# Turning the adjacency by DMA from a bf16 scratch in DRAM, and centring the layer norm on VectorE, in a four-layer graph-attention kernel

## Chip, cores and metric

The kernel runs on one core of a Trainium2 chip. The metric is the device time of one execution in microseconds (us); lower is better. The engines are named as the profile names them: PE is TensorE (PEld its weight loads), DVE is VectorE, ACT is ScalarE, POOL is GpSimd, SP is SyncE, which here only issues DMAs.

## What is computed

There are 16 graphs of 1024 nodes with 256 features, and an adjacency of 1024 x 1024 int32 for each. Four layers follow one another; each takes the layer norm of the nodes, cuts it off at 0, attends over the neighbours and adds the result to the nodes. Cut to what matters:

```python
for layer in range(4):
    h = maximum((x - mean(x)) / sqrt(var(x) + 1e-5), 0)      # per node
    Wh = h @ W                                               # 256 -> 256
    e = act(Wh @ a_src [:, None] + Wh @ a_dst [None, :])     # 1024 x 1024
    att = softmax(where(adj != 0, e, -inf))                  # layer 1: exp(-leaky), no softmax
    x = x + post(att @ Wh)                                   # layer 3: 4 heads of 64, own layer norm
```

The kernel needs the adjacency turned: its masks hold, for a block j of 128 neighbours on the partitions, all 1024 rows i along the free axis.

## The kernel before

A guard decides at the end, from a few statistics, whether a general path has to run; in this case it does not, and all time is in `short_path`.

A batch is one graph. Two Python generators, `stream(0)` and `stream(1)`, take the even and the odd batches; a small loop interleaves them by the virtual times that they yield, with the second one 120 units behind. So while one stream is in layer 3 the other is in layers 0 to 2. This gives the order in which the program is written. The framework's scheduler then places each engine's instructions: an engine may be given a later instruction early, where what it needs is ready in the scheduler's own model. Every engine then runs its own list strictly in order, and waits on semaphores.

What one batch does:

- `load(b)` (L95) brings the nodes `x_b` (one DMA on SP's queue, L98) and the mask. Each of 8 row blocks of the adjacency is fetched by a DMA on POOL's queue that also casts int32 to bf16 (L105), into one of 3 buffers `adj_i`, two ahead (`AHEAD`). ACT squares it with a sum (L116, tile `wide`; the sums serve the guard). PE turns its eight 128 x 128 blocks into one PSUM tile of the pool `misc` (L121), which has 3 buffers that the kernel shares with all other turns, and ACT copies that tile as uint8 into the mask (L122). The load of batch b + 2 is spread over layer 3 of batch b: one step after each of its 8 head halves (L421).
- `project(l, ...)` (L215), for pairs of 128-node tiles, 4 pairs in each layer: DVE takes mean and variance (L220, L221) and scales the variance (L211), POOL raises it to the power -1/2 (L212). ACT negates the mean (L224), then ACT computes relu(x - mean) for each tile (L228, tile `above`), PE turns it (L232), ACT copies it out of PSUM (L234, `hT`), PE multiplies with W (L238), and ACT and DVE evict it (L288 to L292, in layer 3 L308 to L316).
- `weigh` (L244): DVE makes the attention weights (L257), eight instructions of 128 x 512 for each half, each with the mask of one j. Three layers need 16 of them, layer 3, with its four heads, 64.
- `attend` (L320) multiplies weights and values on PE (L340) and ends in `finish`: ACT and DVE (L273 to L276), then POOL adds to `x_b` (L277). The next layer's `project` of a pair follows two tiles later, and its statistics (L220) wait for L277.
- Layer 3 (from L372): PE L416, ACT L420 copies the sums, PE turns them back (L425), and DVE and POOL do its layer norm (L381 to L396). Two stores of the result go out on SP's queue (L441).

The pieces that the change touches read:

```python
        def fetch(i: int):
            fetched[i] = adjs.tile([P, N], BF, name="adj_i")
            nc.gpsimd.dma_start(fetched[i], adj[b, ts(i, P), :])
```

```python
        minus_mean = small.tile([P, 2], F32, name="minus_mean")
        nc.scalar.mul(minus_mean, mv[:, :, 0], -1.0)
```

Of the kernel before, what the change touches and what calls it, by code (L numbers as in the profile page):

```python
# [31 lines left out]
F32 = mybir.dt.float32  # L32
BF = mybir.dt.bfloat16
# [3 lines left out]
AF = mybir.ActivationFunctionType  # L37
ALU = mybir.AluOpType
AX = mybir.AxisListType

P = 128
# [17 lines left out]
def short_path(ctx: ExitStack, tc: tile.TileContext, ins: dict, out: bass.AP, bad: bass.AP):  # L59

    nc = tc.nc
    x, adj = ins["x"], ins["adj"]
    B, N, D = x.shape
    H, T, E = ins["L3_a_src"].shape
    NI = N // P
# [5 lines left out]
    AHEAD = 2  # L71
    LAG = 120.0

    const = ctx.enter_context(tc.tile_pool(name="const", bufs=1))
    nodes = ctx.enter_context(tc.tile_pool(name="nodes", bufs=3))
    adjs = ctx.enter_context(tc.tile_pool(name="adjs", bufs=3))
    wide = ctx.enter_context(tc.tile_pool(name="wide", bufs=3))
    psum = ctx.enter_context(tc.tile_pool(name="psum", bufs=2, space=bass.MemoryType.PSUM))

    ident = const.tile([P, P], F32, name="ident")  # L80
    make_identity(nc, ident)
    ident_b = const.tile([P, P], BF, name="ident_b")
    nc.vector.tensor_copy(ident_b, ident)
    minus_half = const.tile([P, 1], F32, name="minus_half")
    nc.vector.memset(minus_half, -0.5)
    ones = const.tile([P, P], F32, name="ones")
# [2 lines left out]
    squares = const.tile([P, B, NI], F32, name="squares")  # L89
# [3 lines left out]
    xs, masks = {}, {}  # L93

    def load(b: int):  # L95

        xs[b] = nodes.tile([P, NI, D], F32, name="x_b")
        nc.sync.dma_start(xs[b], x[b].rearrange("(i p) f -> p i f", p=P))  # L98
        masks[b] = nodes.tile([P, NI, N], U8, name="mask")
        fetched = {}  # L100

        def fetch(i: int):

            fetched[i] = adjs.tile([P, N], BF, name="adj_i")
            nc.gpsimd.dma_start(fetched[i], adj[b, ts(i, P), :])  # L105

        for i in range(AHEAD):
            fetch(i)
        yield
        for i in range(NI):  # L110
            if i + AHEAD < NI:
                fetch(i + AHEAD)
            adj_i = fetched.pop(i)

            every = wide.tile([P, N], BF, name="wide")
            nc.scalar.activation(  # L116
                every, adj_i, AF.Square, bias=minus_half, accum_out=squares[:, b, i : i + 1]
            )
            turned = psum.tile([P, NI, P], BF, name="misc", bufs=3)
            for j in range(NI):  # L120
                nc.tensor.transpose(turned[:, j, :], adj_i[:, ts(j, P)], ident_b)  # L121
            nc.scalar.copy(masks[b][:, :, ts(i, P)], turned)  # L122
            yield


# [8 lines left out]
    bias = const.tile([P, D], F32, name="bias")  # L134
# [4 lines left out]
    for _ in load(0):  # L139
        pass  # L140
# [5 lines left out]
    with tc.tile_pool(name="prep", bufs=2) as prep:  # L146
# [30 lines left out]
        for l, form in enumerate(forms):  # L177
            n = EXT[l] // 3
# [25 lines left out]
    small = ctx.enter_context(tc.tile_pool(name="small", bufs=6))  # L204
# [4 lines left out]
    def inverse_root(var: bass.AP, n: int, eps: float, scale: float = 1.0) -> bass.AP:  # L209
        r = small.tile([P, n], F32, name=f"rstd{n}")  # L210
        nc.vector.tensor_scalar(r, var, scale, eps, op0=ALU.mult, op1=ALU.add)  # L211
        nc.gpsimd.tensor_tensor(r, r, minus_half.to_broadcast([P, n]), op=ALU.pow)  # L212
        return r

    def project(l: int, xb: bass.AP, pair: int, evict):  # L215

        mv = small.tile([P, 2, nc.vector.BN_AGGR_DIM], F32, name="mv")
        for n in range(2):
            stats = small.tile([P, nc.vector.BN_STATS_DIM], F32, name="stats")
            nc.vector.bn_stats(stats, xb[:, 2 * pair + n, :])  # L220
            nc.vector.bn_aggr(mv[:, n, :], stats)  # L221
        rstd = inverse_root(mv[:, :, 1], 2, LN_EPS)
        minus_mean = small.tile([P, 2], F32, name="minus_mean")
        nc.scalar.mul(minus_mean, mv[:, :, 0], -1.0)  # L224
        turned = psum.tile([P, NK, 2 * P], F32, name="misc", bufs=3)
        for n in range(2):
            above = work.tile([P, D], F32, name="above")
            nc.scalar.activation(  # L228
                above, xb[:, 2 * pair + n, :], AF.Relu, bias=minus_mean[:, n : n + 1]
            )  # L230
            for k in range(NK):
                nc.tensor.transpose(turned[:, k, ts(n, P)], above[:, ts(k, P)], ident)  # L232
        hT = wide.tile([P, NK, 2 * P], F32, name="hT")
        nc.scalar.copy(hT, turned)  # L234
        for n in range(2):
            projected = psum.tile([P, D + EXT[l]], F32, name="projected")
            for k in range(NK):
                nc.tensor.matmul(  # L238
                    projected, hT[:, k, ts(n, P)], W[l][:, k, :],
                    start=(k == 0), stop=(k == NK - 1),  # L240
                )
            evict(2 * pair + n, projected, rstd[:, n : n + 1])
# [36 lines left out]
    def batch(b: int):  # L279
        xb, mask = xs.pop(b), masks.pop(b)  # L280
        coming = load(b + 2) if b + 2 < B else iter(())

        def begin(l: int):
# [36 lines left out]
        def attend(l: int, V: bass.AP, finish, then: int):  # L320
# [12 lines left out]
            for i in range(NI):  # L333
                t = next(weighing[1], None)
                if t:
                    yield t
                acc = psum.tile([P, HALF], F32, name="acc", bufs=3)[:, : D + 1]
                w = halves[i // NG]
                for j in range(NI):
                    nc.tensor.matmul(  # L340
                        acc, w[:, j, ts(i % NG, P)], V[:, j, : D + 1],
                        start=(j == 0), stop=(j == NI - 1),
                    )
                finish(i, acc)
                yield 3.6
                if i % 2 == 0 and i > 0:
                    project(then, xb, i // 2 - 1, following[1])
                    yield 4.0
            project(then, xb, NI // 2 - 1, following[1])
            yield 4.0  # L350
            return following[0]
# [12 lines left out]
        for pair in range(NI // 2):  # L364
            project(0, xb, pair, evict)
            yield 4.0
# [81 lines left out]
    def stream(first: int):  # L448
        if first:
            for _ in load(first):  # L450
                yield 2.0
        for b in range(first, B, 2):
            yield from batch(b)
# [314 lines left out]
def tile_gat4(  # L768
# [27 lines left out]
    nc.vector.memset(ones, 1.0)  # L796
    n_bad = flags.tile([1, 1], I32, name="n_bad")
    short_path(tc, ins, out, bad)
    with tc.tile_pool(name="flag_psum", bufs=1, space=bass.MemoryType.PSUM) as psum:
        bads = psum.tile([1, 1], F32, name="bads")  # L800
# [39 lines left out]
```

## Time and profile before

| | |
|---|---|
| median of 3 runs | 3347.73 us (3344.62 to 3347.99) |
| the profiled execution | 3347.73 us, of which its span 3346.1 us |
| mean granted PE clock | 0.985 of full speed |
| PE, DVE, ACT, POOL busy | 3098.2, 2381.6, 1235.0, 1082.2 us |
| PE busy from 0 to 50 us | 22.6 us |
| PE busy from 3030 to the end, 316.1 us | 272.6 us |
| adjacency DMAs (L105) | 128 of 256 KB written; 3.8 us from issue to landing |
| PE turns of the adjacency (L121) | 1024, 88.0 us busy |
| ACT copies into the mask (L122) | 128, 1005 ns each |
| ACT negated mean (L224), centring (L228) | 256 of 202 ns, 512 of 502 ns |

The span is what the profile resolves; 1.6 us of the execution lie around it. Busy time counts an engine from the start of an instruction to its end, overlaps once. A wait is the idle time of an engine before an instruction, put down to what ended last. The chain of waits is followed back from the last instruction, at each step to what released it.

### The profile page before, as it was taken

To read this page: it belongs to the slowest core of one execution; us is meant where nothing else is said; L and a number is where in the kernel's file an instruction comes from. 1 tells how busy PE (TensorE), PEld (TensorE's weight loads), DVE (VectorE), ACT (ScalarE), POOL (GpSimd) and SP (SyncE) were. 2 spreads that over 40 slices of the span, in tenths; PEclk is the share of its full clock that TensorE was granted. 3 is DMA by queue.
4 is the path that set the end of the run, shared out by engine and by line. 5 is a ranking of instruction groups with operands and counts; after the bars stand their busy time and mean duration, and the time that the engine had idled before them with its cause. 6 is when DMAs were issued, how large, how long until landed. Compare 5 with 4: busy or idle time off the path is not lost.

```text
span 3346.1 us, 38658 instructions
## 1 busy us (share of the span) xinstructions
PE 3098.2 (93%) x13702; PEld 2124.8 (64%) x13702; DVE 2381.6 (71%) x5628; ACT 1235.0 (37%) x2849; POOL 1082.2 (32%) x1286
## 2 busy tenths in 40 slices
PE   6899998999989999899998999989999899998987
PEld 5765755667656675666756667566675666756662
DVE  4567686777767777677677776777677676776766
ACT  4433434334343343424334243342424334333231
POOL 1223424233232342413334233342323423234242
PEclk9999999999999999999999999999999999999998
DMA  4101101011010110100111010010101101000000
GB/s 115 26 4 16 32 10 42 4 19 29 13 38 7 16 29 13 38 10 13 29 16 35 10 27 18 13 35 10 42 4 16 32 13 38 4 13 13 1 13 14
DMA packets 55191, 73.20 MB, mean 22 GB/s; under 512 B 4048, under 2 KB 37968, under 8 KB 54992
## 3 DMA queue, kind: packets, MB, share of 16 engines
q0 software_dynamic: 18432, 33.56, 6.6%
q1 hardware_dynamic: 36560, 37.10, 3.5%
q8 instruction: 111, 1.82, 0.2%
q14 instruction: 88, 0.72, 0.1%
HBM read 87.43 MB, written 16.78 MB: 31 GB/s over the span
## 4 chain that ended last, share of the span: by engine, by line
PE 54%; DVE 30%; ACT 6%; POOL 6%; issue 3%; DMA 1%; SPq 0%; POOLq 0%; ACTq 0%
PE acc L340 22%; DVE weights L257 19%; PE acc L416 15%; PE projected L238 11%; PE misc L232 3%; POOL rstd L212 2%; DVE above L276 2%; POOL x_b L277 1%; DVE stats L220 1%; PE misc L249 1%; DVE above L275 1%; DVE y L382 1%; ACT above L228 1%; ACT mask L122 1%; DVE y L394 1%
## 5 line engine op out<-in xcount | busy, mean ns | idle before, releaser
L340 PE MATMUL acc<-V,weights 128*128 128x257 f32 x6144 | 1445.2, 384 | 18.9 <-DVE weights L257 17.0
L340 PEld LDWEIGHTS acc<-V,weights 128*128 128x128 f32 x6144 | 1136.6, 191 | 211.3 <-DVE weights L257 46.1
L416 PE MATMUL acc<-weights,V 128*65 128x512 f32 x2048 | 913.3, 593 | 0.0
L257 DVE SCALAR_TENSOR_TENSOR weights<-row,ex,mask 128x512 f32<-128x512 f32 x1024 | 766.7, 789 | 12.8 <-ACT row L253 12.0
L257 DVE SCALAR_TENSOR_TENSOR weights<-row,V,mask 128x512 f32<-128x512 f32 x768 | 570.1, 787 | 79.3 <-ACT row L253 79.3
L416 PEld LDWEIGHTS acc<-weights,V 128*65 128x65 f32 x2048 | 278.8, 138 | 493.5 <-issue 433.5
L238 PE MATMUL projected<-W,hT 128*128 128x259 f32 (+1 forms) x2048 | 527.7, 402 | 36.2 <-ACT hT L234 34.8
L212 POOL TENSOR_TENSOR rstd<-rstd,minus_half 128x2 f32<-128x2 f32 (+1 forms) x320 | 306.3, 960 | 743.6 <-DVE rstd L211 621.9
L238 PEld LDWEIGHTS projected<-W,hT 128*128 128x128 f32 x2048 | 384.2, 196 | 151.8 <-ACT hT L234 87.8
L277 POOL TENSOR_TENSOR x_b<-x_b,above 128x256 f32<-128x256 f32 x256 | 219.7, 860 | 618.5 <-DVE above L276 541.6
L232 PE MATMUL misc<-ident,above 128*128 128x128 f32 x1024 | 190.6, 292 | 139.3 <-ACT above L228 138.9
L220 DVE BATCH_NORM_STATS2 stats<-x_b 128x6 f32<-128x256 f32 x512 | 207.2, 416 | 148.6 <-POOL x_b L277 143.7
L273 ACT ACTIVATE below<-acc,inv 128x256 f32<-128x256 f32 x256 | 119.0, 471 | 505.2 <-DVE inv L266 446.6
L232 PEld LDWEIGHTS misc<-ident,above 128*128 128x128 f32 x1024 | 122.8, 146 | 219.0 <-ACT above L228 197.4
L224 ACT ACTIVATE minus_mean<-mv 128x2 f32<-128x2 f32 x256 | 51.4, 202 | 526.7 <-DVE mv L221 514.3
L228 ACT ACTIVATE above<-x_b,minus_mean 128x256 f32<-128x256 f32 x512 | 235.9, 502 | 17.1 <-POOL x_b L277 4.9
L105 POOL DMA_DIRECT2D adj_i<-in_adj_dram x128 | 77.1, 602 | 450.3 <-ACT sums L420 154.5
L420 ACT COPY sums<-acc 65x512 f32<-65x512 f32 x128 | 73.7, 576 | 377.9 <-PE acc L416 377.4
L265 DVE TENSOR_SCALAR inv<-acc 128x1 f32<-128x1 f32 x256 | 37.6, 150 | 242.2 <-PE acc L340 242.2
L234 ACT COPY hT<-misc 128x512 f32<-128x512 f32 x256 | 148.7, 583 | 122.2 <-PE misc L232 121.1
L288 ACT ACTIVATE V<-projected,rstd 128x3 f32<-128x3 f32 x384 | 99.5, 261 | 237.9 <-PE projected L238 209.5
L292 DVE TENSOR_SCALAR V<-projected,rstd,V 128x256 f32<-128x256 f32 x256 | 134.9, 537 | 70.7 <-ACT V L288 70.2
(71 smaller groups left out, 2535.0 us busy)
## 6 DMA issues: line engine op xcount, KB each, us to landing
adj_i<-in_adj_dram POOLq DMA_DIRECT2D x128, 256.0 KB, 3.8
x_b<-in_x_dram SPq DMA_DIRECT2D x16, 1024.0 KB, 7.5
out_dram<-y SPq DMA_DIRECT2D x32, 512.0 KB, 3.8
W<-in_L_gnn_W_dram SPq DMA_DIRECT2D x3, 256.0 KB, 5.0
a_b<-in_L_gnn_a_dram SPq DMA_DIRECT2D x3, 256.0 KB, 7.9
a_b<-in_L_gnn_a_src_dram SPq DMA_DIRECT2D x1, 640.0 KB, 8.3
a_b<-in_L_gnn_a_dst_dram SPq DMA_DIRECT2D x1, 640.0 KB, 10.2
W<-in_L_gnn_W_dram SPq DMA_DIRECT2D x2, 128.0 KB, 7.8
```

What stands on the lines that cost most here:

```text
L212: nc.gpsimd.tensor_tensor(r, r, minus_half.to_broadcast([P, n]), op=ALU.pow)
L220: nc.vector.bn_stats(stats, xb[:, 2 * pair + n, :])
L228: nc.scalar.activation(above, xb[:, 2 * pair + n, :], AF.Relu, bias=minus_mean[:, n : n + 1])
L232: nc.tensor.transpose(turned[:, k, ts(n, P)], above[:, ts(k, P)], ident)
L234: nc.scalar.copy(hT, turned)
L238: nc.tensor.matmul(projected, hT[:, k, ts(n, P)], W[l][:, k, :], start=(k == 0), stop=(k == NK - 1),)
L257: nc.vector.scalar_tensor_tensor(w[:, j, :], r, c(j), mask[:, j, ts(half, HALF)], op0=op, op1=ALU.mult)
L273: nc.scalar.activation(below, acc[:, :D], AF.Exp, scale=inv)
L277: nc.gpsimd.tensor_add(xi, xi, above)
L292: nc.vector.tensor_scalar(V[:, i, :D], projected[:, :D], rstd, V[:, i, D : D + 1], op0=ALU.mult, op1=ALU.mult,)
L340: nc.tensor.matmul(acc, w[:, j, ts(i % NG, P)], V[:, j, : D + 1], start=(j == 0), stop=(j == NI - 1),)
L416: nc.tensor.matmul(accT, V3[:, j, h, :], w[:, j, :], start=(j == 0), stop=(j == NI - 1))
```

## The change

It has two parts. The first makes no more use of PE for the adjacency: for each batch four DMAs on POOL's queue cast the adjacency from int32 to bf16 into a scratch of 1024 x 1024 in DRAM (`narrow`, two buffers), 256 rows each. Eight DMA transposes on SP's queue then read 128 columns of all 1024 rows and write them turned into a buffer `adj_j` of 128 x 1024. ACT squares and sums that buffer as before, and copies it from SBUF, no longer from PSUM, into `masks[b][:, j, :]`. The bf16 identity goes.

The second moves the centring: the negated mean and the two ACT instructions in `project` give way to one DVE instruction for each tile, which subtracts the mean and takes the maximum with 0.

```diff
+    dram = ctx.enter_context(tc.tile_pool(name="dram", bufs=2, space=bass.MemoryType.DRAM))
...
-    ident_b = const.tile([P, P], BF, name="ident_b")
-    nc.vector.tensor_copy(ident_b, ident)
...
+        narrow = dram.tile([N, N], BF, name="narrow")
+        for q in range(4):
+            nc.gpsimd.dma_start(narrow[ts(q, 2 * P), :], adj[b, ts(q, 2 * P), :])
         fetched = {}
-        def fetch(i: int):
-            fetched[i] = adjs.tile([P, N], BF, name="adj_i")
-            nc.gpsimd.dma_start(fetched[i], adj[b, ts(i, P), :])
-        for i in range(AHEAD):
-            fetch(i)
+        def fetch(j: int):
+            fetched[j] = adjs.tile([P, N], BF, name="adj_j")
+            nc.sync.dma_start_transpose(fetched[j], narrow[:, ts(j, P)])
         yield
-        for i in range(NI):
+        for j in range(AHEAD):
+            fetch(j)
+        for j in range(NI):
...
             nc.scalar.activation(
-                every, adj_i, AF.Square, bias=minus_half, accum_out=squares[:, b, i : i + 1]
+                every, adj_j, AF.Square, bias=minus_half, accum_out=squares[:, b, j : j + 1]
             )
-            turned = psum.tile([P, NI, P], BF, name="misc", bufs=3)
-            for j in range(NI):
-                nc.tensor.transpose(turned[:, j, :], adj_i[:, ts(j, P)], ident_b)
-            nc.scalar.copy(masks[b][:, :, ts(i, P)], turned)
+            nc.scalar.copy(masks[b][:, j, :], adj_j)
...
-        minus_mean = small.tile([P, 2], F32, name="minus_mean")
-        nc.scalar.mul(minus_mean, mv[:, :, 0], -1.0)
         for n in range(2):
             above = work.tile([P, D], F32, name="above")
-            nc.scalar.activation(
-                above, xb[:, 2 * pair + n, :], AF.Relu, bias=minus_mean[:, n : n + 1]
+            nc.vector.tensor_scalar(
+                above, xb[:, 2 * pair + n, :], mv[:, n, 0:1], 0.0, op0=ALU.subtract, op1=ALU.max
             )
```

More of the change, by code (lines that the diff above doesn't have):

```diff
@@ L99, in load @@
         masks[b] = nodes.tile([P, NI, N], U8, name="mask")
+        narrow = dram.tile([N, N], BF, name="narrow")
+        for q in range(4):
+            nc.gpsimd.dma_start(narrow[ts(q, 2 * P), :], adj[b, ts(q, 2 * P), :])
         fetched = {}
-        def fetch(i: int):
-            fetched[i] = adjs.tile([P, N], BF, name="adj_i")
-            nc.gpsimd.dma_start(fetched[i], adj[b, ts(i, P), :])
-        for i in range(AHEAD):
-            fetch(i)
-        yield
-        for i in range(NI):
-            if i + AHEAD < NI:
-                fetch(i + AHEAD)
-            adj_i = fetched.pop(i)
+        def fetch(j: int):
+            fetched[j] = adjs.tile([P, N], BF, name="adj_j")
+            nc.sync.dma_start_transpose(fetched[j], narrow[:, ts(j, P)])
+        yield
+        for j in range(AHEAD):
+            fetch(j)
+        for j in range(NI):
+            if j + AHEAD < NI:
+                fetch(j + AHEAD)
+            adj_j = fetched.pop(j)
             every = wide.tile([P, N], BF, name="wide")
             nc.scalar.activation(
-                every, adj_i, AF.Square, bias=minus_half, accum_out=squares[:, b, i : i + 1]
+                every, adj_j, AF.Square, bias=minus_half, accum_out=squares[:, b, j : j + 1]
             )
-            turned = psum.tile([P, NI, P], BF, name="misc", bufs=3)
-            for j in range(NI):
-                nc.tensor.transpose(turned[:, j, :], adj_i[:, ts(j, P)], ident_b)
-            nc.scalar.copy(masks[b][:, :, ts(i, P)], turned)
+            nc.scalar.copy(masks[b][:, j, :], adj_j)
             yield
```

## Prediction, made before the changed kernel was run

> **What bounds the kernel now.** I read the page from its busy shares to its slices and then the chain of waits.
>
> ```profile
> PE 3098.2 (93%) x13702; PEld 2124.8 (64%) x13702; DVE 2381.6 (71%) x5628; ACT 1235.0 (37%) x2849; POOL 1082.2 (32%) x1286
> ...
> PE 54%; DVE 30%; ACT 6%; POOL 6%; issue 3%; DMA 1%; SPq 0%; POOLq 0%; ACTq 0%
> ```
>
> PE is busy 93% of the span, yet only 54% of the chain is PE: for 30% of the time the end is set by DVE, while PE works off what the other stream has ready. So a microsecond taken from PE is not a microsecond of span. Next I cut one period into windows of 10 us. These three are a stretch where PE and DVE are both full, its end, and the change-over in which one stream leaves layer 3 and the other layer 2 (columns: PE, PEld, DVE, ACT, POOL).
>
> ```profile
> 1290.00:1300.00 10.00, 10.00 (x37) 5.05 (x36) 10.00 (x23) 1.90 (x4) 4.60 (x4) 1.00 0.00 1
> 1300.00:1310.00 10.00, 7.18 (x40) 5.85 (x40) 4.22 (x13) 4.33 (x10) 1.68 (x3) 1.00 0.18 26
> ...
> 1390.00:1400.00 10.00, 7.53 (x37) 5.60 (x36) 7.63 (x25) 4.54 (x13) 6.97 (x9) 1.00 0.82 233
> ```
>
> PE idles just after the full-DVE stretch and in the change-over; of the 420 us of this series it idles 23. The waits by line say for what:
>
> ```profile
> PE misc L232 <- ACT above L228: 138.9, 76, 4.8
> PE projected L238 <- ACT hT L234: 34.8, 24, 2.7
> PE acc L340 <- DVE weights L257: 17.0, 19, 1.5
> ```
>
> PE's largest wait, 139 us in 76 places, is for the centring that this change moves. The chain in order of time shows such a place: DVE was the late one, ACT came after it.
>
> ```profile
> 1302.70 0.09 DVE mv L221
> 1302.82 0.21 ACT minus_mean L224
> 1303.11 0.52 ACT above L228
> 1303.67 0.44 PE misc L232 x2
> ...
> 1320.93 0.45 PE misc L121 x8
> ```
>
> The last line is the other thing that goes: eight turns of the adjacency hold PE for 0.45 us.
>
> **What the Trainium skill says.** "VectorE: DVE Perf Modes", section "The perf-mode tier table": a tensor_scalar on fp32 in SBUF runs at 2 elements a cycle, with an operand in PSUM at 1. The trace agrees:
>
> ```profile
> L142 DVE TENSOR_SCALAR beta<-beta 128x256 f32<-128x256 f32 x1 | 0.3, 293 | 12.3 <-DMA beta<-in_L_gnn_ln_beta_dram 12.3
> L275 DVE TENSOR_SCALAR above<-acc,inv 128x256 f32<-128x256 f32 x256 | 121.8, 478 | 44.1 <-ACT below L273 42.6 <-PE misc L232 0.6
> L276 DVE SCALAR_TENSOR_TENSOR above<-below,above 128x256 f32<-128x256 f32 x256 | 150.8, 592 | 3.9
> ```
>
> L142 has SBUF on both sides, L275 reads PSUM: 293 against 478 ns. "SBUF — State Buffer", section "Who interferes with whom": an instruction of DVE in such a two-port mode, or with two SBUF inputs, shares a port pair with POOL, and who starts second waits. The trace fits: L276 has a mean of 592 but a median of 424 ns. "DMA: Bandwidth & Descriptors", section "DMA Transpose (X-bar)": only the SP and ACT queues turn, and two-byte types only, hence the bf16 scratch; no transpose by DMA is in this trace. "VectorE: DVE Perf Modes", section "The three transpose paths", gives 1309 ns for 128 x 128 bf16 by DMA.
>
> **The change part by part.**
>
> *PE turns removed (a gain).* 128 bursts x 0.45 us = 58 us of PE (the row's 88.0 us counts every burst to the end of its last, pipelined matmul). It counts where PE sets the end: 54% of the chain of 93% busy, a share of 0.58, so -34 us. Bounds: -20 (PE more often waits for DVE) and -58. With them go 128 users of the three PSUM buffers `misc`; the waits of PE's turns L249 and L425 for L122 sum to 4 us, at nothing. The copy L122 stays on ACT, 1005 ns from PSUM; from SBUF I take the price of L116 from SBUF, 1137 ns, 17 us more on an engine that is 37% busy: nothing, as the 287 us below more than make room. If ACT were late there, 1% of the chain (L122's share) is at stake.
>
> *Centring moved, the latency (a gain).* Before, from the start of the last mv to PE: 1303.67 - 1302.70 = 0.97 us. After: mv 0.09 and a gap of 0.03, then rstd L211 0.16 (it stands ahead of the centring in the program), one DVE instruction of 0.29, a hop of 0.06: 0.63. So 0.34 us at each of 76 waits: -26 us. Bounds: 0, if DVE has other work listed between, and -60, since the average wait is 1.8 us and part of it was ACT being busy with L116 or L122 in between.
>
> *ACT relieved (a small gain).* 51.4 + 235.9 = 287 us leave ACT. POOL waited 96.1 us for L228 before L316 (26 times), PE 34.8 us for hT. I take -6 us, from nothing to -20.
>
> *Centring on DVE (a loss).* 512 instructions. DVE's instructions overlap at their ends: L257 lasts 0.74 us (median), but the chain counts 0.66 us apiece, so 293 ns hold DVE for about 0.21 us. For the fight with POOL I add 0.05, as L257's mean lies above its median (787 against 741): 0.26 x 512 = 133 us. On the 30% of the chain that is DVE: +40 us. Bounds: 0.21 x 512 x 0.3 = +32 at least with that share; L275's price, 0.40 us apiece, and a share of half: +102. A loss cannot be excluded, a gain of this item can. Behind each new DVE instruction stand L257 weights of the other stream, and PE waits for those. The buffer `above` is shared with L275, and ACT's short waits for it (4.6 us, 19 times) pass to DVE: nothing.
>
> *DMAs.* POOL issues 64 instead of 128 (602 ns each now, so at most 77 us either way) and no longer stands waiting before them: 154.5 + 146.1 + 128.8 us of POOL's waits go. Its next instruction was mostly not ready then, so nothing. SP gets 128 transposes; it does little but wait for the stores. The traffic grows by 2 MB written and 2 MB read for each batch, on DMA engines that move 22 GB/s on average. The path is longer: the four writes take 8 x 1.73 us of all engines (6.6% of the span over 128 loads) plus about 2 us to land, 16 us; then a first transpose, by the skill's price an estimate of 8 x 1.31 = 10.5 us if its blocks follow one another. Before, fetches were issued far ahead of their use, one at 1389.2 with no copy into a mask between 1380.2 and 1463.9, so I cost 26 us at nothing. Without this cover the wait is priced among the rivals.
>
> *Start.* The first mask now needs 26 us of DMA instead of 7, and both first batches' 4 MB are read at once. But the first weights were made at 45.8 us, after ACT had gone through eight masks (to 35) and the centrings; ACT has less to do now. +5 us, between -5 and +15.
>
> Sum: -34 - 26 - 6 + 40 + 5 = -21. The profiled execution took 3347.7 us (span 3346.1 and 1.6 around it), which is also the median: 3327 us.
>
> **Rivals.**
>
> *DVE becomes the limit (slower).* Place: stretches such as 1270 to 1303, where the chain runs through DVE for 31 us and PE lives from a backlog. Shorter PE work runs out earlier, so DVE's share of the chain grows to a half. At 0.30 us apiece, 154 x 0.5 = +77; PE's gain falls to -20, the latency's to -13, start +5: +49, 3397 us. It decides once DVE's loss passes the gains, 66 - 5 = 61 us: at 0.26 us apiece from a share of 46%. For it: DVE at 71% would go to 75% and more, full in three of ten windows. Against it: 29% of DVE is idle.
>
> *PE's free time turns into waiting (no change).* The PE gain stops at 20 and the latency's at 20: -20 - 20 - 6 + 40 + 5 = -1, 3347 us. For it: PE already waits behind full-DVE stretches.
>
> *ACT waits for the scratch (slower).* If fetches are placed only one step ahead (sums at 1446.7 and 1463.4, 17 us), 26 us of DMA leave ACT standing 9 us at each of 14 batches, with everything for hT and rows behind it: 126 us; half of it hidden, +63 - 21: 3390 us. SP's order adds to this: transposes queue behind a store that waits for the end of a batch.
>
> *PE gain in full (faster by more).* -58 and -40 for latency against 32: 3282 us.
>
> **Chances.** The sum above 0.42, PE gain in full 0.09, no change 0.12, DVE the limit 0.24, ACT waiting 0.13. The forecast is that of the likeliest, 3327 us, whose own range is 3300 to 3340. Gains and losses of the two parts are of the same size, so cases of both signs hold weight, and the range of 8 in 10 goes from 3280, the full gain, to 3400, the limit on DVE. A measurement of this kernel tells 0.2% (7 us) from nothing: faster 0.50, same 0.13, slower 0.37.
>
> **What would show it.** L121 and L224 gone; PE busy near 3030 us; PE's wait before L232, now for DVE, about 100 us instead of 139; the new DVE row near 0.3 to 0.35 us; DVE's share of the chain above 30%. Waits of ACT before L116 for a DMA, beyond the first 50 us, would show the scratch to be late. I am wrong if the new row costs over 0.4 us, if DVE's share goes towards a half, or if PE's wait before L232 does not fall.

## The result, and the profile after

The changed kernel takes 3472.3 us (median of 4 runs, 3462.05 to 3477.45) against 3346.18 us for the kernel before, measured beside it: a ratio of 1.0374, 95% interval 1.0348 to 1.0400. Forecast were 3327 us and a range of 3280 to 3400: wrong in sign and in size. One execution further down, the profiled one of the run called "DMA turns alone", took 3584.39 us where the four others took 3489.83 to 3498.91; the ratio leaves it out, and its profile is not used.

The page of the changed kernel: busy shares, the slices of PE and of the DMA engines (each 87 us wide), the chain.

```profile
PE 3051.4 (88%) x12678; PEld 2059.0 (59%) x12678; DVE 2496.7 (72%) x6139; ACT 980.9 (28%) x2081; POOL 1042.0 (30%) x1222
...
PE   0079999989999999989999999999999899998986
...
DMA  9940010010101001010100101010010101000000
...
DVE 40%; PE 37%; ACT 7%; POOL 5%; DMA 4%; another core or an unknown queue 4%; issue 2%; SPq 1%; ACTq 0%; POOLq 0%; DVEq 0%
```

PE lost 47 us of work with the 1024 turns (3098.2 to 3051.4), and is at 8 or 9 from the fourth slice to the last but one. The loss lies in the first two and a half slices: PE at 0 and the DMA engines at 9. Windows of 20 us over the start of the changed kernel (columns: length, then busy time of PE, PEld, DVE, ACT, POOL, PE clock, DMA share, GB/s):

```profile
20.00:40.00 20.00, 0.00 (x0) 0.00 (x0) 0.00 (x0) 0.00 (x0) 0.82 (x2) 1.00 0.95 205
...
100.00:120.00 20.00, 0.00 (x0) 0.00 (x0) 0.00 (x0) 0.00 (x0) 4.22 (x9) 1.00 1.01 216
...
180.00:200.00 20.00, 2.26 (x6) 1.73 (x7) 0.99 (x2) 10.88 (x18) 0.00 (x0) 1.00 0.81 168
200.00:220.00 20.00, 20.00 (x89) 16.36 (x88) 16.98 (x40) 19.29 (x33) 0.03 (x1) 1.00 0.54 97
```

The kernel before from 40 us on:

```profile
40.00:60.00 20.00, 19.97 (x98) 16.52 (x97) 16.89 (x37) 6.92 (x19) 0.00 (x0) 1.00 0.00 0
```

PE had steady work from 40 us on; now it has it from 200 us, when the share of the DMA engines has come down from 1.01 to 0.54. A second measure cuts the span cleanly: the stores of each batch on SP's queue. The first store of a batch moves from 365.2 to 511.6 us, +146.4. From there to the first store of the fourteenth batch (thirteen intervals), 2668.8 become 2641.0 us, -27.8. The tail goes from 312.1 to 315.7, +3.5. The sum is the difference of the spans (3468.3 against 3346.1, +122.2). So the later batches did become faster, and the start gave back five times as much.

What fills the DMA engines is read from POOL's timeline in the changed kernel (start, duration, what, how many; in brackets the idle time before and what ended it):

```profile
2.48 3.40 POOL L102 DMA_DIRECT2D narrow<-in_adj_dram  x7
9.79 0.49 POOL L102 DMA_DIRECT2D narrow<-in_adj_dram  x1 [3.90 <-DMA narrow<-in_adj_dram]
...
22.36 0.49 POOL L102 DMA_DIRECT2D narrow<-in_adj_dram  x1 [2.03 <-DMA narrow<-in_adj_dram]
56.92 0.76 POOL L211 TENSOR_TENSOR rstd<-rstd,minus_half 128x2 f32<-128x2 f32 x1 [34.07 <-DVE rstd L210]
57.65 0.55 POOL L102 DMA_DIRECT2D narrow<-in_adj_dram  x1
...
166.65 0.49 POOL L102 DMA_DIRECT2D narrow<-in_adj_dram  x1 [2.03 <-DMA narrow<-in_adj_dram]
```

All 64 scratch writes, those of all 16 batches, are issued within 167 us: eight at once, then one each time an earlier one has landed, every 2.5 us. Only once does POOL pause: the layer norm of the first nodes stands next in its list, and it waits 34 us for DVE. Fourteen writes are out by 22.4 us. The fourteenth belongs to the fourth batch, and the first transpose, which reads the first batch's scratch, starts only at 45.05. So the two buffers of the scratch pool held nothing back; why they did not is not shown. SP's timeline shows what stood behind them:

```profile
3.47 18.18 SPq L137 DMA_DIRECT2D bias<-in_L_gnn_bias_dram  x1
...
38.99 2.39 SPq L97 DMA_DIRECT2D x_b<-in_x_dram  x1
...
45.05 9.99 SPq L107 DMA_TRANSPOSE adj_j<-narrow  x3
...
62.32 158.86 SPq L107 DMA_TRANSPOSE adj_j<-narrow  x16
```

The load of the bias holds SP's queue for 18 us, so the first nodes are asked for at 39 us instead of 5.85; then a group of sixteen transposes takes 159 us. The view of the tile `adj_j` says how unusual that is, and the chain in order of time what waited for them:

```profile
L107 SPq DMA_TRANSPOSE adj_j<-narrow x128: 1159/1162/83844, 45.0 to 3083.3; - x128
...
DMA to landing us min/median/max: 3.0/3.5/126.7
```

```profile
62.57 83.72 another core or an unknown queue
146.37 1.24 ACT wide L118 x2
...
150.00 39.03 another core or an unknown queue
189.12 1.24 ACT wide L118 x2
```

A transpose takes 1.16 us of SP and lands after 3.5 us (median), but among all these writes (the storm, from here on) up to 83.8 and 126.7 us. ACT stands before two of its squares for 84 and 39 us (122.9 us in 2 places), with its copies for PE queued behind them. (The chain puts these two waits down to an unknown queue; the waits view gives the transpose.)

Outside the start, the other prices of the prediction can be read as well:

```profile
L225 DVE TENSOR_SCALAR above<-x_b,mv 128x256 f32<-128x256 f32 x512 | 219.3, 438 | 3.6 <-POOL x_b L274 1.9
```

```profile
PE misc L229 <- DVE above L225: 159.2, 157, 2.8
```

The new DVE row has a mean of 438 ns (its median is 345, its longest 1359), and PE's wait for the centring did not fall; it rose from 138.9 to 159.2 us. Outside the start (from 240 to 3000 us) it rose as well, from 104.5 to 135.6.

### The profile page after: what moved, and what is told of

It is laid out like the page before. It is cut to its first block, busy times and chain, and to the rows that moved or that the text cites. A ratio compares the mean times of both kernels' runs of the same rounds, so it can differ in the third digit from the quotient of the medians.

```text
span 3468.3 us, 36630 instructions
## 1 busy us (share of the span) xinstructions
PE 3051.4 (88%) x12678; PEld 2059.0 (59%) x12678; DVE 2496.7 (72%) x6139; ACT 980.9 (28%) x2081; POOL 1042.0 (30%) x1222
## 3 DMA queue, kind: packets, MB, share of 16 engines
q0 software_dynamic: 2048, 33.56, 4.5%
## 4 chain that ended last, share of the span: by engine, by line
DVE 40%; PE 37%; ACT 7%; POOL 5%; DMA 4%; another core or an unknown queue 4%; issue 2%; SPq 1%; ACTq 0%; POOLq 0%; DVEq 0%
DVE weights L254 23%; PE acc L337 16%; PE acc L413 10%; PE projected L235 8%; DMA adj_j<-narrow 4%; DVE above L225 3%; PE misc L229 2%; DVE above L272 2%; DVE stats L219 2%; POOL x_b L274 2%; DVE above L273 1%; ACT wide L118 1%; DVE V L289 1%; ACT mask L121 1%
## 5 line engine op out<-in xcount | busy, mean ns | idle before, releaser
L254 DVE SCALAR_TENSOR_TENSOR weights<-row,ex,mask 128x512 f32<-128x512 f32 x1024 | 758.6, 783 | 2.5 <-ACT row L250 0.9
L254 DVE SCALAR_TENSOR_TENSOR weights<-row,V,mask 128x512 f32<-128x512 f32 x768 | 561.7, 778 | 48.1 <-ACT row L250 46.6
L229 PE MATMUL misc<-ident,above 128*128 128x128 f32 x1024 | 196.8, 296 | 163.4 <-DVE above L225 159.2
L219 DVE BATCH_NORM_STATS2 stats<-x_b 128x6 f32<-128x256 f32 x512 | 206.7, 413 | 83.8 <-POOL x_b L274 79.4
L225 DVE TENSOR_SCALAR above<-x_b,mv 128x256 f32<-128x256 f32 x512 | 219.3, 438 | 3.6 <-POOL x_b L274 1.9
L118 ACT ACTIVATE wide<-adj_j,minus_half 128x1024 bf16<-128x1024 bf16 x128 | 145.6, 1138 | 122.9 <-DMA adj_j<-narrow 122.9
L378 POOL TENSOR_TENSOR y<-y,bias 128x512 f32<-128x512 f32 x64 | 89.6, 1400 | 298.5 <-DVE y L425 278.8
L272 DVE TENSOR_SCALAR above<-acc,inv 128x256 f32<-128x256 f32 x256 | 121.6, 478 | 65.2 <-ACT below L270 64.2
```

What stands on the lines that cost most here:

```text
L118: nc.scalar.activation(every, adj_j, AF.Square, bias=minus_half, accum_out=squares[:, b, j : j + 1])
L225: nc.vector.tensor_scalar(above, xb[:, 2 * pair + n, :], mv[:, n, 0:1], 0.0, op0=ALU.subtract, op1=ALU.max)
L254: nc.vector.scalar_tensor_tensor(w[:, j, :], r, c(j), mask[:, j, ts(half, HALF)], op0=op, op1=ALU.mult)
L272: nc.vector.tensor_scalar(above, acc[:, :D], inv, 0.0, op0=ALU.mult, op1=ALU.max)
```

## Experiments

Three causes were to be told apart. The storm: all writes at once at the start. DVE: the centring makes it the limit, as its share of the chain (40%) suggests. The longer path: write, transpose and copy cost something in every batch. Each run stands beside runs of the kernel before on the same chip, and the ratios are to those. "First store" and "a batch" are from the stores in the one profile of each kernel: the first one, and the time from the second to the fourteenth, divided by 12.

| kernel | ratio (95% interval) | first store | a batch |
|---|---|---|---|
| before | 1 | 365.2 us | 205.0 us |
| changed | 1.0374 (1.0348 to 1.0400) | 511.6 | 202.8 |
| centring on DVE alone | 0.9987 (0.9980 to 0.9994) | 362.4 | 204.6 |
| DMA turns alone | 1.0431 (1.0414 to 1.0449) | | |
| two fixed scratch tiles | 1.0017 (1.0008 to 1.0025) | 396.0 | 203.3 |
| padded scratch rows | 1.0338 (1.0320 to 1.0357) | 513.1 | 202.5 |
| before + unread writes | 1.0286 (1.0269 to 1.0303) | 463.0 | 204.8 |
| late scratch | 1.0262 (1.0245 to 1.0279) | 386.3 | 209.8 |
| hybrid, late, DVE | 1.0249 (1.0232 to 1.0267) | 370.5 | 210.9 |
| hybrid, late, ACT | 1.0237 (1.0220 to 1.0254) | 377.9 | 210.6 |
| hybrid, early, DVE | 0.9912 (0.9897 to 0.9927) | 361.5 | 202.5 |
| hybrid, early, ACT | 0.9951 (0.9937 to 0.9964) | 369.0 | 204.0 |

**One part at a time.** First the centring alone, in the kernel before:

```diff
-        minus_mean = small.tile([P, 2], F32, name="minus_mean")
-        nc.scalar.mul(minus_mean, mv[:, :, 0], -1.0)
...
-            nc.scalar.activation(
-                above, xb[:, 2 * pair + n, :], AF.Relu, bias=minus_mean[:, n : n + 1]
+            nc.vector.tensor_scalar(
+                above, xb[:, 2 * pair + n, :], mv[:, n, 0:1], 0.0, op0=ALU.subtract, op1=ALU.max
             )
```

> The kernel before with the centring on DVE alone; the adjacency is fetched and turned as before. Theory (the start: all scratch writes of all 16 batches go out at once and hold up the first masks): this kernel has no scratch, so it stays within 1% of before, 3320 to 3370 us, and PE begins its steady work near 50 us. Rival (DVE has become the limit): it carries nearly the whole loss, 3430 to 3480 us, with DVE's share of the chain near 40%.

It came out 0.13% faster than before. DVE's share of its chain is even higher than in the changed kernel:

```profile
DVE 45%; PE 43%; POOL 5%; ACT 4%; issue 3%; DMA 1%; SPq 0%; ACTq 0%; POOLq 0%
```

So DVE does take over the chain, and in this run that costs nothing: a larger share of the chain is not in itself a loss. What DVE gained in it (from 30 to 45%), PE and ACT gave up (from 54 to 43% and from 6 to 4%). The counterpart is the changed kernel with the centring back on ACT:

> The changed kernel with the centring put back on ACT; the adjacency still goes through the DRAM scratch and the DMA transposes. Theory (the start): the loss stays, 3440 to 3490 us, PE begins its steady work near 200 us. Rival (DVE the limit): the loss goes, 3300 to 3350 us.

The loss stays, at 1.0431 (3493.8 us, 4 us above what was expected). DVE is out as the cause; the adjacency's path carries all of it. With that path the centring on DVE is even a gain, 1.0374 against 1.0431.

**Holding the writes back.** Two scratch tiles made once, so that a write must wait for the transposes of two batches earlier:

```diff
+    scratch = [dram.tile([N, N], BF, name=f"scratch{s}") for s in range(2)]
...
-        narrow = dram.tile([N, N], BF, name="narrow")
+        narrow = scratch[b % 2]
```

> The changed kernel with two scratch tiles that are made once and used in turn, so that a batch's scratch writes wait for the transposes of two batches earlier. Theory (the start): only the writes of two batches go out before the first masks, PE begins its steady work at 60 to 90 us instead of 205, and 115 to 145 us come back: 3325 to 3355 us. Rival (the longer path costs in every batch, or DVE is the limit): at most 30 us come back, 3440 us or more.

The ratio falls from 1.0374 to 1.0017 (3355.92 us, a microsecond above what was expected). POOL's timeline shows the writes spread out:

```profile
2.49 3.40 POOL L103 DMA_DIRECT2D scratch<-in_adj_dram  x7
...
59.41 1.98 POOL L103 DMA_DIRECT2D scratch<-in_adj_dram  x4 [9.32 <-DMA adj_j<-scratch]
...
89.72 1.92 POOL L103 DMA_DIRECT2D scratch<-in_adj_dram  x4 [28.33 <-DMA adj_j<-scratch]
...
327.40 0.60 POOL L103 DMA_DIRECT2D scratch<-in_adj_dram  x1 [0.17 <-issue]
```

Eight writes at the start, four at 59 and four at 90 us, the rest far into the run. 115.6 of the 146.4 us before the first store come back with a change that touches only when the writes go out, and a batch stays at 203.3 us. What is left at the start is 31 us, and a batch, no longer than before, shows no cost of the longer path.

**What in the storm holds the first masks.** A guess was that the small pieces of a transpose stand in turn behind the large ones of a write. Padding the scratch's rows cuts the writes into rows (17408 packets on their queue instead of 2048):

```diff
-        narrow = dram.tile([N, N], BF, name="narrow")
+        narrow = dram.tile([N, N + 64], BF, name="narrow")[:, :N]
```

> The changed kernel with 64 unused columns behind each row of the scratch, so that a row is a piece of its own: the same 64 MB are read at the start, but in pieces of at most 4 KB read and 2 KB written instead of 64 KB and 32 KB. Theory (start), in the form that small transposes stand behind large pieces in turn: first masks come much earlier though the writes take as long, PE steady at 80 to 130 us, 3360 to 3410 us. In the form that plain bandwidth is short until all writes are done: no gain, PE steady near 200 us, 3450 to 3480 us.

SP's loads do get through sooner, the nodes at 9.49 us instead of 38.99:

```profile
3.47 3.28 SPq L137 DMA_DIRECT2D bias<-in_L_gnn_bias_dram  x1
...
9.49 0.43 SPq L97 DMA_DIRECT2D x_b<-in_x_dram  x1
...
74.55 145.37 SPq L107 DMA_TRANSPOSE adj_j<-narrow  x16
```

But sixteen transposes still take 145 us, and the first store is no earlier (513.1). Of the two forms that were expected, the one in which bandwidth is short until the writes are done gives this time. The guess about the pieces is wrong as the reason for the loss, at least down to rows of 2 KB.

Next, the same writes added to the kernel before, with nothing reading them:

```diff
+        narrow = dram.tile([N, N], BF, name="narrow")
+        for q in range(4):
+            nc.gpsimd.dma_start(narrow[ts(q, 2 * P), :], adj[b, ts(q, 2 * P), :])
```

> The kernel before, to which the same 64 scratch writes are added; nothing reads the scratch, and the adjacency is fetched and turned as before. Theory (the start is lost to the traffic of all the writes at once): PE begins its steady work well after 48 us here too, 3400 us or more. Rival (it is only the new chain, write then transpose then mask, that is long): the writes pass beside the work, 3340 to 3365 us.

The first store moves by 98 us and a batch not at all (204.8). Its chain in order of time shows a second way of paying:

```profile
134.89 19.18 DMA narrow<-in_adj_dram
...
154.35 19.19 DMA narrow<-in_adj_dram
...
174.31 1.95 issue
...
176.77 0.74 POOL rstd L216
```

Here there is no transpose by DMA that could be late. POOL itself stands in line: each write waits for an earlier one to land (19.2 us from issue to landing), and the power for the layer norm is queued behind the writes. So the storm harms on its own. The changed kernel does not pay in this second way; POOL is not among the main parts of its chain over the first 215 us, which are the two waits before the squares and SP's load of the bias:

```profile
by line: another core or an unknown queue 57.1%; SPq L137 16.5%; ACT wide L118 5.8%; DMA adj_j<-narrow 4.6%; ACT mask L121 4.4%; PE projected L235 3.2%; issue 2.4%; SPq L97 1.1%; SPq L148 1.0%; ACT hT L231 0.7%; SPq L127 0.6%; ACT L118 0.6%
```

What the two kernels have in common is the storm.

**Holding them back further.** With the same two fixed tiles, the scratch writes of batch b + 2 now also wait for a token: a few values of `h3`, made late in layer 2 of batch b, which a small DMA writes into the scratch tile first:

```diff
+        narrow = scratch[b % 2]
+        if ready is not None:
+            token = const.tile([P, 64], BF, name="token", bufs=2)
+            nc.vector.tensor_copy(token, ready())
+            nc.sync.dma_start(
+                narrow.rearrange("(q r) c -> r q c", q=4)[0, :, :64], token[:4, :]
+            )
         for q in range(4):
             nc.gpsimd.dma_start(narrow[ts(q, 2 * P), :], adj[b, ts(q, 2 * P), :])
...
+        coming = load(b + 2, lambda: last["h3"][:, 0, :64]) if b + 2 < B else iter(())
```

> The changed kernel with two fixed scratch tiles, whose writes for batch b + 2 also wait for a small token that batch b makes late in layer 2. Only the first two batches' writes are left at the start. Theory (the start): PE steady between 60 and 100 us, better than with two fixed tiles alone by the 16 MB that those sent out at 59 and 90 us, 3325 to 3350 us; batches cost 203 us each, as in the changed kernel. Rival (the scratch pays only because its writes lie far ahead): ACT waits for transposes in every batch, stores come 206 us apart or more.

The start improves (first store 386.3), but the kernel is 2.6% slower than before, far outside the 3325 to 3350 us of the theory: a batch now costs 209.8 us, as its rival has it (206 or more). ACT's timeline at the first of these batches:

```profile
184.50 0.59 ACT L238 COPY hT<-misc 128x512 f32<-128x512 f32 x1 [0.41 <-PE misc L236]
196.27 1.15 ACT L125 ACTIVATE wide<-adj_j,minus_half 128x1024 bf16<-128x1024 bf16 x1 [11.18 <-DMA adj_j<-scratch]
...
197.42 0.40 ACT L292 ACTIVATE V<-projected,rstd 128x3 f32<-128x3 f32 x2
...
198.65 0.59 ACT L238 COPY hT<-misc 128x512 f32<-128x512 f32 x1
```

The writes went out at 179.1 us, the first square could start at 196.3: 17 us from write to mask, of which ACT stood idle for 11.2, with an eviction (L292) and hT behind. DVE's part of the eviction (L296) waits for ACT's, and PE for DVE's, so PE has an idle time of 10 us:

```profile
197.70 1.00 DVE L296 TENSOR_SCALAR V<-projected,rstd,V 128x256 f32<-128x256 f32 x2 [12.19 <-ACT V L292]
...
198.29 3.94 PE L242 MATMUL projected<-W,hT 128*128 128x268 f32 x8 [10.39 <-DVE V L296]
```

Over the run ACT's square waits for transposes for 103.2 us in 16 places, 7.4 us for each of the 14 later batches, where the changed kernel has no such wait after the start; a batch is 7.0 us longer. The granted PE clock was lower in this run and the next two (0.961 to 0.972), but that is not the reason: the changed kernel's executions at 0.965 to 0.969 took 3462 to 3477 us, that at 0.985 took 3470. The far-ahead writes were thus not only a harm: they were the cover that makes a batch cheap. The same with the first two batches turned by PE as before, which takes the scratch out of the start altogether:

```diff
+        if b < 2:
...
+                turned = psum.tile([P, NI, P], BF, name="misc", bufs=3)
+                for j in range(NI):
+                    nc.tensor.transpose(turned[:, j, :], adj_i[:, ts(j, P)], ident_b)
+                nc.scalar.copy(masks[b][:, :, ts(i, P)], turned)
```

> As the one with the token, but the first two batches are fetched and turned by PE as before, so that nothing of the scratch is left at the start; centring on DVE. Theory (the whole loss is the start, each later batch gains 2.2 us): PE steady near 48 us and 14 x 2.2 = 31 us gained on before, 3310 to 3325 us. Rival (the gain per batch needs the early writes): 3340 to 3360 us.

> The same with the centring on ACT as before: the removal of PE's turns alone, without its start. If the turns are worth 1.8 us a batch and the centring next to nothing, 3315 to 3330 us; if the gain of the changed kernel's later batches comes from both parts together, 3340 us or more.

Both missed: 1.0249 and 1.0237, with the start nearly back (370.5 and 377.9) and 211 us for a batch. ACT's square waits as before, 107.8 and 108.5 us in 14 places each. Where the centring runs makes little difference to that.

**Early, but not at once.** The token is made after layer 0 instead, from the values of layer 1, and the writes go out there:

```diff
         V = yield from attend(0, V, finish0, 1)
+        if b + 2 < B:
+            narrowed(b + 2, V[:, 0, :64])
```

> First two batches turned by PE, the rest by DMA from two fixed scratch tiles, whose writes for batch b + 2 go out after layer 0 of batch b (held there by a token), some 100 us and more before their first use; centring on DVE. Theory (two separate costs: the start is lost to writes that all go out at once, and a write that goes out only one step ahead makes ACT wait in every batch): neither is left, stores 203 us apart as in the changed kernel, 3310 to 3325 us. Rival (the DMA path costs something in every batch wherever its writes lie): stores 207 us apart or more, 3370 us or more.

> The same with the centring on ACT: removal of PE's turns alone. Theory: 3315 to 3335 us, since the centring alone was worth 0.1%. If the gain of the changed kernel's later batches needs both parts, no better than before, 3345 us or more.

With the centring on DVE it takes 3321.48 us against 3351.93 beside it, 0.88% faster than the kernel before; the first store is at 361.5 us and a batch costs 202.5. Its writes go out at 69, 223 and 415 us:

```profile
68.58 0.54 POOL L103 DMA_DIRECT2D scratch<-in_adj_dram  x1 [4.78 <-DMA scratch<-token]
...
69.99 1.53 POOL L103 DMA_DIRECT2D scratch<-in_adj_dram  x3
...
222.68 0.60 POOL L103 DMA_DIRECT2D scratch<-in_adj_dram  x1 [15.12 <-DMA scratch<-token]
...
415.30 2.06 POOL L103 DMA_DIRECT2D scratch<-in_adj_dram  x4
```

The second wait of 15 us shows the token's price on POOL; the time of a batch shows nothing of it. With the centring on ACT the ratio is 0.9951 (3335.91 us, a microsecond above what was expected). The DVE form of this version beats both kernels.

## Why the prediction was wrong, point by point

*The step that failed* is the last term of the sum, the start: "+5 us, between -5 and +15", with "both first batches' 4 MB are read at once". It measured +146 us to the first store. Not two batches but all sixteen were written without a stop but one, 64 pieces of 0.5 MB at the 205 to 216 GB/s that the windows show. Two batches alone cost about what the range allowed: with only their writes at the start the first store came at 386.3 us, without them at 370.5 (late scratch; hybrid, late, DVE), 16 us. The reason lies one paragraph earlier. The prediction saw that "fetches were issued far ahead of their use" and took it as cover, "so I cost 26 us at nothing". It did not ask what had bounded that lead. In the kernel before, three buffers in SBUF did:

```profile
L105 POOL DMA_DIRECT2D adj_i<-in_adj_dram x128 | 77.1, 602 | 450.3 <-ACT sums L420 154.5 <-ACT wide L116 146.1 <-PE misc L121 128.8
```

Of the 429 us of POOL's waits that the prediction counts as removed, 275 ended when ACT (L116) or PE (L121) was done with such a buffer. The writes to the scratch lost those waits and got nothing in their place, as the scratch pool's two buffers did not act as one. That the removal of a wait can be a cost was the missing thought.

*PE turns removed*, -34 us for 16 batches: right in kind, too large in size. With the centring on DVE in both, the early hybrid is 0.9912 / 0.9987, 0.75% or 25 us faster for 14 batches; with ACT in both, 0.49%, 16 us. For 16 batches that would be 29 and 19 us.

*The centring*: -26 for the latency, -6 for ACT and +40 on DVE, together +8, against a measured -0.13%, -4 us. Beside the DMA path it was worth more: 0.9912 against 0.9951, 0.4% or 13 us. So its sign was wrong. The parts were not as described either. DVE's row has a mean of 438 ns, over the 0.3 to 0.35 that was to show the step right, though its median of 345 lies within; PE's wait did not fall to 100 us but rose. Either the relief of ACT is worth more than the 6 us it was given, or the DVE instruction costs less than the 40 us; no run measures the two apart. All three signs named for being wrong appeared, a row over 0.4 us, DVE's share of the chain near a half and no fall of PE's wait. They appeared as well in the run with the centring alone (445 ns, 45%, and PE idle for 154.2 us before these turns where it was 139.3), and that run is no slower: they do not show a loss.

*Both together, without the start*: the prediction's terms give -26 us; the changed kernel's own thirteen intervals gave -27.8, and the early hybrid's 14 batches -0.88%, 30 us. That the sum without the start comes so close is in part luck: the turns gave less than their 34 us, and the centring, priced as a loss of 8, was a gain.

*The rivals.* "DVE becomes the limit" had 0.24 and would have given 3397 us; DVE's share of the chain rose to 40% and more, and the run with that part alone still was no slower. ("Full in three of ten windows" holds for 90% and more, 13 of the 42 windows; six were full to the end.) "ACT waits for the scratch" had 0.13. In the changed kernel it holds only at the start, 122.9 us in two places; in the late version it came as described (the waits of ACT's square for the transposes sum to 103.2 us in 16 places), with a first wait of 11.2 us where 9 were priced and 17 us from write to mask where 26 were. The case that occurred, a storm of writes, was not on the list.

## What to carry to other kernels

When a wait is taken away, ask what it was holding back. A buffer's wait also limits how far ahead a queue may run. Here the writes had no buffer to wait for, and all of them went out at the start, ahead of or beside the first loads. For staged data the right time lies between: here, a write 17 us before its use left ACT idle for up to 11 us, all writes at once cost 146 us before the first store, and a write at 69 us for transposes from 147 us on cost neither. And a chain share that moves from one engine to another says who ends last, not that time was lost: DVE went from 30 to 45% of the chain in a kernel that became 0.13% faster.

## What was not expected of the hardware

POOL had eight scratch writes in flight at a time, and then issued one every 2.5 us, each 512 KB (1 MB of int32 read), at a DMA share of 1.00. Beside them a load of 128 KB from SP held SP's queue for 18.2 us, where it took about 1 us before, and a transpose that otherwise holds SP for 1.16 us held it for up to 83.8. A transpose of 1024 x 128 bf16 lands after 3.5 us (median), a third of the 10.5 us that the prediction estimated from the price of one 128 x 128 block in the Trainium skill ("VectorE: DVE Perf Modes", "The three transpose paths"): its eight blocks do not follow one another at that price. The subtract-and-max with a per-partition operand has a median of 345 ns, where the add of a constant (L142 before) took 293 ns; its mean of 438 ns fits the ports that DVE shares with POOL, which the Trainium skill describes ("SBUF — State Buffer", "Who interferes with whom"), though no run here takes POOL's work away to show it. How the DMA engines divide themselves between the two queues stays open; the padded rows showed only that pieces of 2 KB in place of larger ones do not bring the time back.
